# Two attention layers and a sign layer on one core: row stores, first score operands, adjacency padding and five sums of products moved

## The chip, the cores and the metric

One core of a Trainium2 chip. The metric is the device time of one execution in microseconds. The engines are named as the profile names them: PE (TensorE's matmuls; PEld, its weight loads), DVE (VectorE), ACT (ScalarE), POOL (GpSimd), SP (SyncE, which here only issues DMA transfers; SPq is its queue).

## The reference

x is 3327 x 512, adj a 3327 x 3327 matrix of zeros and ones. Two attention layers with residual, a layer norm, then a layer of signs, another residual and another layer norm:

```
for l in range(2):                                   # h starts as x
    Wh, Ws = split(h @ W_stack[l])                   # 3327 x 512 each
    a = softmax(Wh @ Ws.T, axis=-1) * adj
    h = leaky_relu(a @ Wh + h, 0.01)
x = layernorm(x + h)
ba, bw = (x > 0), sign(weight)
out = layernorm(x + relu(adj @ (ba @ bw.T)))
```

## The kernel before

**Tiles.** The 3327 rows are 26 tiles of 128 (the last has 127 rows), 13 pairs of tiles (`q`, `g`) and 7 chunks of four tiles (`c`; the last chunk has two). Every large product is done in Strassen's way: seven half-size products instead of eight, from sums of blocks that DVE or POOL make (`left_sums`, `right_sums`: four operations each).

**Projection** (`project`, lines 285 to 488). Chunk by chunk, PE makes `wsT` and then `whT`, each a "weave" of two chains of seven products. `weave` (line 222) takes several lists and emits their entries in the order of (i + 0.5) / length, so that other work stands between the products. Into the weave of chunk c+1's `wsT` goes the list `rest` of chunk c: the sums of the scores' right operands (`queries`, stored by POOL as `gs_d`) and, for each tile, `turn_rows` (line 417): two DVE transpositions (line 422) into a buffer `wr`, of which there are three, and at once four stores of it on SP (line 427). Into the weave of `whT` goes `keys` (the scores' left operands, stored by POOL as `xs_d`) and, for the first six value pairs, `sum_values`: four DVE sums of rows that `begin_values` loaded back with three transfers on SP; two POOL stores keep the result in `ws_d`. Pairs 0 and 1 are loaded after chunk 1, 2 and 3 after chunk 2, 4 and 5 after chunk 3, and summed a chunk later. The first chunk of layer 0 is turned by PE (`transpose_first`); weights are put in place by ACT (`part_w`).

**Attention** (`attention`, lines 499 to 1081). The loop variable v counts the pairs (g, q) whose values are being multiplied; u = v + 30 counts half steps of the scores, which run 30 steps ahead. Before v = 0 PE does scores only: 14 products for each q of a chunk, from `gs` (seven blocks for a chunk, two buffers) and `xs` (for each q two tiles, `xs0` and `xs1`, two buffers each, loaded by `load_xs`, line 515). The first `gs` is loaded at u = -4 in one transfer of 1792 KB, each `xs` two half steps ahead. Then DVE subtracts the column maximum (`off`), ACT takes the exponential, DVE multiplies with the adjacency (`masked`), POOL makes four sums (lines 738 to 741, `as`), and PE multiplies with the values (line 765). `load_adj` (line 659) loads 256 x 256 blocks of adj into four buffers; where a block reaches past column 3326 (g = 12) or row 3326 (q = 12), POOL first sets the missing part to zero (lines 664 and 666), and the last tile's load comes in pieces of 128, 112 and 15 rows. A list `early` places other work at given v: the value pairs that projection did not do (the last seven, `begin_values` and `sum_values`, lines 913 and 917), and in layer 0 the next layer's weights and first four tiles of x, at the end (lines 968 to 976).

**The end of layer 1.** From v = 130 on, `load_products` (line 1085) loads the sign layer's operands `xw` and, at v = 158 to 168, calls `product_sums` (line 1109) for pairs 0 to 10: four DVE subtractions each, written over the values `wh[p]` that are no longer needed. PE does parts of the last product (`aggregate`) between the values. `finale` does the rest.

**What sets the order.** Both functions run under a manual schedule: within each, every engine runs its instructions in the order in which the program emits them. Only where projection and attention meet does the scheduler merge the two orders.

Of the kernel before, what the change touches and what calls it, by code (L numbers as in the profile page):

```python
# [30 lines left out]
def kernel(  # L31
# [199 lines left out]
    ch_lane, acc_lane = (ps_ch, "ch"), (ps_acc, "acc")  # L231
    w_rows, wb_of, wsum_of, spare_of, x_first, sums_first = ({} for _ in range(6))
    ROWS = 6

# [32 lines left out]
    def right_x(c, xT, t):  # L267
# [7 lines left out]
        )  # L275

    def load_values(l, q, b12):

        nc.sync.dma_start(out=wh[q][:, 0], in_=wh_d[l][2 * q][:, :HD])
        nc.sync.dma_start(  # L280
            out=wh[q][:, 1:3], in_=wh_d[l][2 * q + 1].rearrange("p (a n) -> p a n", a=2)
        )
        nc.sync.dma_start(out=b12, in_=wh_d[l][2 * q][:, HD:])

    def project(l, pre):
# [3 lines left out]

        def load_x(c, tiles=None):  # L290
            if c >= NC:
                return
            for t in tiles or tiles_of(c):
                some = src[t * P : t * P + rows(t), :]
                if c == 0:
                    xt = slot([P, D], F32, f"xr_{l}_{t}")
                    load_rows(nc.sync, xt, some, rows(t))
                else:
                    xt = slot([P, P // B, P], F32, f"xr_{l}_{t}")
                    if rows(t) < P:  # L300
                        nc.gpsimd.memset(xt[:, rows(t) // B :], 0.0)
                    load_laid(nc.sync, xt, some, rows(t))
                rows_of.setdefault(c, []).append(xt)

        def transpose_first(lane):

            pool, tag = lane
            xTs[0] = pre.tile([P, KD, CW], F32, tag="xT", bufs=2, name=f"xT_{l}_0")
            pts = [pool.tile([P, CW], F32, tag=tag, name=f"pxt_{l}_{k}") for k in range(KD)]
            xts = [t.rearrange("r (p k) -> r k p", k=KD) for t in rows_of[0]]  # L310

            for a in range(CT):
                for k in range(KD):
                    nc.tensor.transpose(pts[k][:, ts(a, P)], xts[a][:, k], ident)
            for k in range(KD):
                copy_out(k, xTs[0][:, k], pts[k])

        def transpose_x(c, a):
# [20 lines left out]
        if l == 0:  # L339
            load_x(0, (0, 1))  # L340
            load_w(l, 1, (0, 1))
            load_x(0, (2, 3))
            load_w(l, 1, (2, 3))
            load_w(l, 0)
            spare_of[l] = ops.tile([P, 14, HW], F32, tag="gs", name=f"spare_{l}")
            wsum_of[l] = ops.tile([P, 4, 2, HD], F32, tag="gs", name=f"wbsum_{l}")
            wb_of[l] = m[:, 0:2], m[:, 2:4]
        else:
            xTs[0] = x_first[l]
            of_x[0] = sums_first[l]  # L350
# [66 lines left out]
        def turn_rows(t, lo, hi):  # L417
# [3 lines left out]
            for side, half in enumerate((lo, hi)):  # L421
# [3 lines left out]
                )  # L425
            for a in range(P // B):
                nc.sync.dma_start(
                    out=wh_d[l][t][:, ts(a, P)].rearrange("(r v) f -> v r f", v=B),
                    in_=wr[ts(a, B)],
                )  # L430

# [13 lines left out]

        rows34 = {}
        weights = [lambda k=k: part_w(l, 0, k, wa[:, k]) for k in range(KD)] + left_w(of_a)
        if l == 0:
            transpose_first(acc_lane)
            for k in range(KD):  # L450
                part_w(l, 1, k, m[:, k])
            t, b = sums_x(0), left_w(of_b)
            for do in t[:2] + b[:2]:
                do()
            weights = [b[2], t[2], b[3], t[3]] + weights
        else:
            weights += [
                lambda e=e: nc.scalar.copy(m[:, 2 * e : 2 * e + 2], wb_of[l][e]) for e in range(2)
            ]
        rest = []  # L460
        for c in range(NC):
# [12 lines left out]
            later = []  # L474
            old = [q for q in (2 * c - 4, 2 * c - 3) if 0 <= q < ROWS]
            turns += [lambda q=q: sum_values(q) for q in old]
            chains, made = products(c, "whT", of_a)
            weave(*chains, rest, turns)
            rest = queries(c, made)
            for a, e in enumerate(made):  # L480
                rest += [
                    lambda t=t, e=e: turn_rows(t, *e) for t in half_tiles(c * CT // 2 + a)
                ]
            for q in (2 * c - 2, 2 * c - 1):
                if 0 <= q < ROWS:
                    begin_values(q)
        for do in rest:
            do()

# [9 lines left out]
    def attention(l, att):  # L499
# [4 lines left out]
        ahead = [(c, q, s) for c in range(NC) for q in range(NQ) for s in range(2)]  # L504
        sc, top, total, off, adj, acc, gs, xs, ch = ({} for _ in range(9))
        asum, ws, out_, early = {}, {}, {}, {}
        WS = 3

        def load_gs(c, i, n=1):
            if i == 0:  # L510
                gs[c] = ops.tile([P, 7, 2, HW], F32, tag="gs", bufs=2, name=f"gs_{l}_{c}")
            if i <= (T3 if len(halves_of(c)) == 2 else B21):
                nc.sync.dma_start(out=gs[c][:, i : i + n], in_=gs_d[l][c][:, i : i + n])

        def load_xs(c, q):
            if len(halves_of(c)) == 2:
                groups = (S1, 4), (A22, 3)
            else:
                groups = (A11, 4),
            for i, (a, n) in enumerate(groups):  # L520
                t = ops.tile([P, 4 - i, 2, P], F32, tag=f"xs{i}", name=f"xs{i}_{l}_{c}_{q}")
                nc.sync.dma_start(out=t[:, :n], in_=xs_d[l][q][:, a : a + n])
                for e in range(n):
                    xs[c, q, a + e] = t[:, e]

        def product(c, q, bank, a, b, start):
# [3 lines left out]
            for k in range(2):  # L530
                nc.tensor.matmul(  # L531
                    ch[bank], xs[c, q, a][:, k], gs[c][:, b, k],
                    start=(start and k == 0), stop=(k == 1), skip_group_check=True,
# [87 lines left out]
        def column_max(g):  # L621
# [27 lines left out]
            def back():  # L649
# [4 lines left out]
                    whole.unsqueeze(2).to_broadcast([P, w, B]),  # L654
                )

            return [(-0.04, fold), (0.2, turn), (0.5, across), (0.7, back)]

        def load_adj(g, q):
            i0, n = half_cols(g)  # L660
            at = att.tile([P, 2, HW], F32, tag="adj", bufs=4, name=f"adj_{l}_{g}_{q}")
            adj[g, q] = at
            if n < HW:
                nc.gpsimd.memset(at[:, :, n:], 0.0)
            if rows(2 * q + 1) < P:
                nc.gpsimd.memset(at[:, 1], 0.0)
            if rows(2 * q + 1) == P:
                nc.sync.dma_start(
                    out=at[:, :, :n],
                    in_=adjT[2 * q * P : (2 * q + 2) * P, i0 : i0 + n].rearrange(  # L670
                        "(a p) i -> p a i", p=P
                    ),
                )
                return
            for a in range(2):
                j = 2 * q + a
                load_rows(
                    nc.sync, at[:, a, :n],
                    adjT[j * P : j * P + rows(j), i0 : i0 + n], rows(j),
                )  # L680

# [242 lines left out]

        for n, q in enumerate(range(ROWS, NQ)):
            at = 1 - LOOK + 4 * n
            assert at + 2 < 1 - WS
# [15 lines left out]
        else:  # L943
# [26 lines left out]

            place(end + 3, 0.9, lambda: load_w(l + 1, 1))
            place(end + 4, 0.2, begin_w)
# [7 lines left out]
            for i in range(4):  # L980
                place(end + 10 + i, 0.65, lambda: parts.pop(0)())
            place(n - 10, 0.95, lambda: load_w(l + 1, 0))
            for a in range(CT):
                place(n - 9 + a, 0.9, lambda a=a: load_first(a))
                place(n - 5 + a // 2, 0.45, lambda a=a: turn_x(x_first[l + 1], a, laid.pop(0)))
# [18 lines left out]
        for v in range(-LOOK - 4, len(steps)):  # L1004
# [6 lines left out]
            if v + 4 in blocks and (v + 4 < 0 or blocks[v + 4] != steps[v + 4]):  # L1011
                load_adj(*blocks[v + 4])
            if 0 <= u + 2 < len(ahead):
                c, q, h = ahead[u + 2]
                if h == 0:
                    load_xs(c, q)
            if u == -4:
                load_gs(0, 0, 7)

# [31 lines left out]
            if last:  # L1051
                load_products(v)
        if not last:
# [23 lines left out]
    JL = 2  # L1077
    NS = -(-NQ // JL)
    EARLY = NQ - 2
    XH = NT // 2  # L1080
# [3 lines left out]

    def load_products(v):

# [15 lines left out]
        p = v - NQ * (NQ - 1) - 2  # L1102
        if 0 <= p < EARLY:
            product_sums(p)
        n = v - NQ * NQ + 3 * NS
        if 0 <= n < 3 * NS:
            load_aggregate(*divmod(n, NS))

    def product_sums(p):
        x1, x2 = xw[2 * p], xw[2 * p + 1]  # L1110
        xt[p] = wh[p].bitcast(F16).rearrange("p a n -> p (a n)")[:, : 4 * HD].rearrange(
            "p (i n) -> p i n", i=4
        )
        for do in right_sums(
            x1[:, :HD], x1[:, HD:], x2[:, :HD], x2[:, HD:], *(xt[p][:, i] for i in range(4))
        ):
# [9 lines left out]
    def aggregate(g, b, p, i):  # L1126
# [9 lines left out]
        else:  # L1136
            of = (t[:, 1], t[:, 2], t[:, 0], x2[:, HD:], t[:, 3])[i - 2]

# [234 lines left out]
```

## Time and profile before

| | us |
|---|---|
| median of 3 runs | 2627.83 (2625.72 to 2629.0) |
| the profiled execution's own time | 2627.48 |
| its span in the trace | 2625.7 |
| PE, PEld busy | 2554.6, 2227.5 |
| DVE, POOL, ACT busy | 2141.6, 1095.4, 802.9 |
| projection of layer 0, up to its last product | 0 to 187 |
| attention of layer 0 | 187 to 1240 |
| projection of layer 1 | 1227 to 1411 |
| attention of layer 1 | 1411 to 2487 |
| rest of the sign layer, up to PE's last matmul | 2487 to 2605.1 |

The page gives busy time per engine; since PE is busy most of the span, the views to read are those that tell when it is not: who waited for whom, and the instructions in order of time around each pause, where the number in brackets is the idle time before an instruction and what ended it. A mean granted clock below 1 in a stretch says that PE ran more slowly there. DMA transfers are issued by SP and POOL in the order of their queues; the trace gives each one's issue and its landing.

### The profile page before, as it was taken

The numbers are of one execution on the slowest core, as the hardware profiler recorded it, in microseconds if no ns is written. First come the engines' busy times: TensorE is split into PE (matmuls) and PEld (weight loads), VectorE is DVE, ScalarE is ACT, GpSimd is POOL, SyncE is SP. The second block draws the span as 40 slices with busy tenths as digits, with TensorE's granted clock in tenths as the row PEclk, the third lists the DMA queues.
The fourth block names the chain that finished last, engine by engine and source line by source line (L and its number), as shares of the span: only waits on it lengthen the run. The fifth ranks groups of instructions, "written<-read, shape, count | busy, mean of one in ns | idle before, by whom it ended". The sixth has DMA issues, their size and how long they took to land. (4 is left out here: it accounts for less than half of the span.)

```text
span 2625.7 us, 40583 instructions
## 1 busy us (share of the span) xinstructions
PE 2554.6 (97%) x12456; PEld 2227.5 (85%) x12456; DVE 2141.6 (82%) x4528; ACT 802.9 (31%) x1986; POOL 1095.4 (42%) x2030
## 2 busy tenths in 40 slices
PE   8979999999999999999998999999999999999998
PEld 7868788888888888887887888888888888888787
DVE  6866888889898888759884888988889888877977
ACT  3323333323333323223322333333323333222143
POOL 3441343444444444557452144444444444455611
PEclk9999999999999999999998999999999999999999
DMA  6888776777777777668788977777787777778775
GB/s 202 302 267 297 267 259 233 249 249 251 249 244 255 242 240 239 233 226 270 227 298 272 345 235 261 236 269 248 247 273 244 265 250 243 247 265 272 260 258 185
DMA packets 366348, 667.77 MB, mean 254 GB/s; under 512 B 52761, under 2 KB 222579, under 8 KB 365868
## 3 DMA queue, kind: packets, MB, share of 16 engines
q1 hardware_dynamic: 329596, 556.00, 65.0%
q0 software_dynamic: 36528, 109.10, 11.0%
q8 instruction: 102, 1.67, 0.3%
q14 instruction: 122, 1.00, 0.1%
HBM read 541.75 MB, written 123.19 MB: 253 GB/s over the span
## 5 line engine op out<-in xcount | busy, mean ns | idle before, releaser
L531 PE MATMUL pZ<-gs,xs 128*128 128x256 f32 x2496 | 640.9, 381 | 30.2 <-DVE whT L190 14.1
L531 PEld LDWEIGHTS pZ<-gs,xs 128*128 128x128 f32 x2496 | 474.7, 191 | 99.4 <-DVE whT L190 14.5
L738 POOL TENSOR_TENSOR as<-s 128x128 f32<-128x128 f32 x338 | 163.3, 483 | 823.5 <-DVE s L700 646.0
L765 PE MATMUL acc<-ws,s 128*128 128x256 f32 x1352 | 402.1, 379 | 0.0
L765 PE MATMUL acc<-wh,s 128*128 128x256 f32 x1352 | 355.9, 379 | 0.9 <-DVE s L700 0.8
L765 PE MATMUL acc<-ws,as 128*128 128x256 f32 x1352 | 348.1, 380 | 8.3 <-POOL as L740 5.6
L531 PE MATMUL pY<-gs,xs 128*128 128x256 f32 x1248 | 320.4, 379 | 0.0
L690 ACT ACTIVATE s<-s 128x512 f32<-128x512 f32 x338 | 213.4, 631 | 283.4 <-DVE s L684 282.2
L765 PEld LDWEIGHTS acc<-ws,as 128*128 128x128 f32 x1352 | 255.9, 190 | 47.2 <-POOL as L740 9.4
L765 PEld LDWEIGHTS acc<-wh,s 128*128 128x128 f32 x1352 | 256.5, 190 | 37.1 <-DVE s L700 2.4
L765 PEld LDWEIGHTS acc<-ws,s 128*128 128x128 f32 x1352 | 256.0, 190 | 34.5
L601 DVE TENSOR_TENSOR top<-top,s 128x512 f32<-128x512 f32 x286 | 199.7, 711 | 82.6 <-ACT s L588 54.3
L531 PEld LDWEIGHTS pY<-gs,xs 128*128 128x128 f32 x1248 | 236.9, 190 | 32.6 <-ACT p L548 0.3
L684 DVE TENSOR_TENSOR s<-s,off 128x512 f32<-128x512 f32 x338 | 248.9, 736 | 0.6
L700 DVE TENSOR_TENSOR s<-s,adj 128x512 f32<-128x512 f32 x338 | 238.3, 705 | 10.2 <-POOL as L740 1.5
L695 DVE TENSOR_TENSOR total<-total,s 128x512 f32<-128x512 f32 x312 | 230.8, 740 | 0.0
L548 ACT COPY u<-pZ 128x256 f32<-128x256 f32 x312 | 115.9, 371 | 358.5 <-PE pZ L531 357.9
L740 POOL TENSOR_TENSOR as<-s 128x128 f32<-128x128 f32 x338 | 201.8, 597 | 26.5
L765 PE MATMUL acc<-wh,as 128*128 128x256 f32 x676 | 201.2, 379 | 0.0
L739 POOL TENSOR_TENSOR s<-s 128x128 f32<-128x128 f32 x338 | 188.6, 558 | 26.5
L741 POOL TENSOR_TENSOR as<-s,as 128x128 f32<-128x128 f32 x338 | 180.2, 533 | 26.5
L573 DVE TENSOR_TENSOR s<-p,u 128x256 f32<-128x256 f32 x156 | 66.4, 426 | 131.0 <-ACT u L548 130.4
(224 smaller groups left out, 3858.8 us busy)
## 6 DMA issues: line engine op xcount, KB each, us to landing
ws<-ws_d SPq DMA_DIRECT2D x338, 512.0 KB, 3.7
xs<-xs_d SPq DMA_DIRECT2D x182, 512.0 KB, 6.0
adj<-in_adjT_dram SPq DMA_DIRECT2D x315, 256.0 KB, 4.3
xs<-xs_d SPq DMA_DIRECT2D x156, 384.0 KB, 6.5
gs<-gs_d SPq DMA_DIRECT2D x74, 256.0 KB, 5.4
adj_d<-ab POOLq DMA_DIRECT2D x169, 112.0 KB, 4.1
ahl<-adj_d SPq DMA_DIRECT2D x78, 224.0 KB, 4.6
xs_d<-s POOLq DMA_DIRECT2D x52, 256.0 KB, 3.6
```

Source lines behind the costliest of these rows:

```text
L531: nc.tensor.matmul(ch[bank], xs[c, q, a][:, k], gs[c][:, b, k], start=(start and k == 0), stop=(k == 1), skip_group_check=True,)
L548: nc.scalar.copy(ch[name], ch[bank])
L601: nc.vector.tensor_tensor(top[i], top[i], t, ALU.max)
L684: nc.vector.tensor_tensor(s, s, off[g].to_broadcast([P, 2, HW]), ALU.subtract)
L690: nc.scalar.activation(sc[g, q], sc[g, q], AF.Exp)
L695: nc.vector.tensor_tensor(total[g], total[g], sc[g, q], ALU.add)
L700: nc.vector.tensor_tensor(s, s, adj[g, q], ALU.mult)
L738: nc.gpsimd.tensor_tensor(s3, a11, a21, ALU.subtract)
L739: nc.gpsimd.tensor_tensor(a21, a21, a22, ALU.add)
L740: nc.gpsimd.tensor_tensor(s2, a21, a11, ALU.subtract)
L741: nc.gpsimd.tensor_tensor(s4, a12, s2, ALU.subtract)
L765: nc.tensor.matmul(acc[g][i // 2][:, i % 2], a[i], b[i], start=(q == 0 and i % 2 == 0), stop=(q == NQ - 1), skip_group_check=True,)
```

## The change

- **Row stores.** `turn_rows` only puts its store on a list; a new entry `store_rows` after it in `rest` issues it, on SP as before. `rest` has 10 entries instead of 6. After the last chunk the stores go to POOL's queue.
- **Value pairs.** Projection does five pairs instead of six: pair c-1 is loaded after chunk c and pair c-2 summed in chunk c. Attention does the other eight, 3 or 4 steps apart instead of 4.
- **First operands of the scores.** `gs` of the first chunk, in seven transfers, and `xs` of q = 0 and 1 are loaded in projection, after chunk 5 of 0 to 6, and no longer in attention. They are emitted before the list with chunk 5's row stores.
- **Adjacency.** No memsets. A block that reaches past the last column is loaded in full width from the flat matrix, so that its last column holds the start of the next row; `off` of that column gets 1e30 by a DVE memset, and since `off` is subtracted the exponential there is zero. The last pair's second tile comes in 112, 14 and 1 rows and a row that fills the padding, and one element more where g = 12: five or six transfers instead of three.
- **Sums of products.** Pairs 0 to 4 are done at v = 143, 145, ... 151 in other buffers; pairs 5 to 10 stay at v = 163 to 168.
- **Start.** Layer 0 loads the four x tiles and then the weights, instead of two and two in turn; `part_w` of a weight follows the copy of the same index.
- **Layer 0's end.** The next layer's weights are loaded one tile per step (from v = 155 and v = 160) instead of four at once at 155 and 159; its four x tiles at v = 155, 157, 159 and 161 instead of 160 to 163.

```diff
-    ROWS = 6
+    ROWS = NC - 2
...
             for k in range(KD):
                 copy_out(k, xTs[0][:, k], pts[k])
+                part_w(l, 1, k, m[:, k])
...
-            load_x(0, (0, 1))
-            load_w(l, 1, (0, 1))
-            load_x(0, (2, 3))
-            load_w(l, 1, (2, 3))
+            load_x(0)
+            load_w(l, 1)
...
-            for a in range(P // B):
-                nc.sync.dma_start(
-                    out=wh_d[l][t][:, ts(a, P)].rearrange("(r v) f -> v r f", v=B),
-                    in_=wr[ts(a, B)],
-                )
+            def store(eng):
+                for a in range(P // B):
+                    eng.dma_start(
+                        out=wh_d[l][t][:, ts(a, P)].rearrange("(r v) f -> v r f", v=B),
+                        in_=wr[ts(a, B)],
+                    )
+            turned.append(store)
+
+        def store_rows(eng=nc.sync):
+            while turned:
+                turned.pop(0)(eng)
...
-            old = [q for q in (2 * c - 4, 2 * c - 3) if 0 <= q < ROWS]
-            turns += [lambda q=q: sum_values(q) for q in old]
+            if 0 <= c - 2 < ROWS:
+                turns.append(lambda: sum_values(c - 2))
...
-                rest += [
-                    lambda t=t, e=e: turn_rows(t, *e) for t in half_tiles(c * CT // 2 + a)
-                ]
-            for q in (2 * c - 2, 2 * c - 1):
-                if 0 <= q < ROWS:
-                    begin_values(q)
+                for t in half_tiles(c * CT // 2 + a):
+                    rest += [lambda t=t, e=e: turn_rows(t, *e), store_rows]
+            if 0 <= c - 1 < ROWS:
+                begin_values(c - 1)
+            if c == NC - 2:
+                gs_of[l] = ops.tile([P, 7, 2, HW], F32, tag="gs", name=f"gs_{l}_0")
+                for i in (B11, B21, T1, T2, B22, T3, T4):
+                    nc.sync.dma_start(out=gs_of[l][:, i], in_=gs_d[l][0][:, i])
+                for q in range(2):
+                    load_xs(l, 0, q)
         for do in rest:
-            do()
+            do() if do is not store_rows else do(nc.gpsimd)
...
+                if half_cols(g)[1] < HW:
+                    nc.vector.memset(off[g][:, 0, half_cols(g)[1] :], -FAR)
...
-            if n < HW:
-                nc.gpsimd.memset(at[:, :, n:], 0.0)
-            if rows(2 * q + 1) < P:
-                nc.gpsimd.memset(at[:, 1], 0.0)
...
+            nc.sync.dma_start(out=at[:, 0], in_=some(j1, P))
+            cut = r - r % 16
+            nc.sync.dma_start(out=at[:cut, 1], in_=some(j2, cut))
+            nc.sync.dma_start(out=at[cut : r - 1, 1], in_=some(j2 + cut, r - 1 - cut))
+            nc.sync.dma_start(out=at[r - 1 : r, 1, :n], in_=some(j2 + r - 1, 1, n))
+            if n < HW:
+                nc.sync.dma_start(out=at[r - 1 : r, 1, n:], in_=some(j2 + r - 2, 1)[:, n:])
+            nc.sync.dma_start(out=at[r:, 1], in_=some(j2, P - r))
...
-            at = 1 - LOOK + 4 * n
+            at = 1 - LOOK + 7 * n // 2
...
-            place(end + 3, 0.9, lambda: load_w(l + 1, 1))
+            for k in range(KD):
+                place(end + 3 + k, 0.9, lambda k=k: load_w(l + 1, 1, [k]))
+                place(end + 8 + k, 0.9, lambda k=k: load_w(l + 1, 0, [k]))
...
-            place(n - 10, 0.95, lambda: load_w(l + 1, 0))
             for a in range(CT):
-                place(n - 9 + a, 0.9, lambda a=a: load_first(a))
+                place(n - 14 + 2 * a, 0.9, lambda a=a: load_first(a))
...
-            if 0 <= u + 2 < len(ahead):
+            if 4 <= u + 2 < len(ahead):
                 c, q, h = ahead[u + 2]
                 if h == 0:
-                    load_xs(c, q)
-            if u == -4:
-                load_gs(0, 0, 7)
+                    load_xs(l, c, q)
...
-        if 0 <= p < EARLY:
+        if SOON <= p < EARLY:
             product_sums(p)
+        p, odd = divmod(v - first[0] - XH, 2)
+        if 0 <= p < SOON and not odd:
+            product_sums(p, att)
...
+        if p < SOON:
+            tags = (("xs1",), ("xs1",), ("top1",), ("p1", "u2"), ("p5", "u3"))[p]
...
+                t = pool.tile([P, n, HD], F16, tag=tag, bufs=2 if tag == "xs1" else 1,
+                              name=f"xsum_{p}_{tag}")
```

Here SOON = 5, NC = 7, NQ = XH = 13, `first[0]` = 130, and `some` takes rows of the flat adjacency in full width.

## The prediction

> **What bounds the kernel now.** I read the page's busy times first.
>
> ```profile
> PE 2554.6 (97%) x12456; PEld 2227.5 (85%) x12456; DVE 2141.6 (82%) x4528; ACT 802.9 (31%) x1986; POOL 1095.4 (42%) x2030
> ```
>
> TensorE is idle for 2625.7 - 2554.6 = 71.1 us. The chain of waits shows its last matmul ending at 2605.1, so 20.6 us of that is a tail that no edit touches. The other 50 us, and time at a lower clock, are all that this change can win: it removes no matmul. Next, who PE waited for (total, times, longest):
>
> ```profile
> PE pZ L531 <- DVE whT L190: 14.1, 2, 7.3
> PE pZ L531 <- DMA xs<-xs_d: 13.1, 6, 5.7
> PE pX_wsT L370 <- DVE whT L190: 5.7, 4, 2.6
> PE pxt L314 <- DMA xr<-in_x_dram: 5.7, 2, 3.8
> PE acc L765 <- POOL as L740: 5.6, 7, 1.2
> ```
>
> The first two rows are four pauses, at the two passages from projection to attention: 7.29 us before 182.15 and 5.74 before 198.52 in layer 0, 6.79 before 1404.89 and 4.45 before 1421.22 in layer 1. The timelines of VectorE and of SyncE's queue say why (start, duration):
>
> ```profile
> 180.89 1.08 DVE L422 STREAM_TRANSPOSE wr<-whT 128x256 f32<-128x256 f32 x2 [8.87 <-DMA wh_d<-wr]
> ```
>
> ```profile
> 161.61 0.34 SPq L513 DMA_DIRECT2D gs<-gs_d  x1
> 162.00 1.71 SPq L522 DMA_DIRECT2D xs<-xs_d  x2
> ...
> 169.47 23.80 SPq L427 DMA_DIRECT2D wh_d<-wr  x24
> 193.32 0.93 SPq L522 DMA_DIRECT2D xs<-xs_d  x2
> ```
>
> Chunk 5's row stores are queued behind the first `gs` (1792 KB) and `xs` (896 KB). A store lands in a median 2.1 us, here in up to 10.2. The fourth turned tile needs a `wr` buffer, of which there are three, and VectorE stands 8.87 us; behind it stands the addition that PE waits for. Then SP must issue eight more stores, chunk 6's, before q=1's `xs` at 193.32: the second pause. The pauses also cost clock (columns: stretch, length, five engines' busy time, granted clock, DMA share, GB/s):
>
> ```profile
> 165.00:181.00 16.00, 9.86 (x89) 9.66 (x87) 6.57 (x17) 4.63 (x17) 5.51 (x10) 0.93 0.99 376
> 179.00:186.00 7.00, 3.85 (x18) 3.68 (x19) 3.03 (x10) 0.53 (x2) 1.96 (x3) 0.53 0.74 229
> 196.00:203.00 7.00, 4.48 (x11) 3.66 (x12) 0.42 (x1) 0.37 (x1) 0.00 (x0) 0.52 0.80 299
> 1400.00:1411.00 11.00, 6.11 (x27) 5.93 (x27) 4.43 (x13) 0.80 (x3) 5.18 (x10) 0.53 0.86 289
> ```
>
> At about half clock, half of PE's busy time is lost: 1.8, 2.1 and 3.0 us, and 1.7 after 1421. With the pauses, passage 0 costs 7.3 + 1.8 + 5.7 + 2.1 = 16.9 us, passage 1 6.8 + 3.0 + 4.5 + 1.7 = 16.0.
>
> **The change, part by part** (gain positive).
>
> *Passages.* Seven `gs` loads and two q's `xs` (2 x 896 KB) now stand on SP at the end of chunk 5, still ahead of its stores; ahead of them come the three loads of value pair 4 (512 KB). q=1's `xs` no longer waits for chunk 6's stores, so the second pause goes: 5.7 + 2.1, and 4.5 + 1.7. What is late next are chunk 5's stores. Pair 4's loads can use 161 to 165, where only 242 GB/s moved; the added 917,000 bytes of `xs` cannot, since DMA is 0.99 busy after that. At all 376 GB/s they take 2.4 us, at half of it, beside POOL's writes, 4.9; I take 3, nearer the first, because POOL's writes are finite and only trade places. VectorE's wait, and PE's, grow by that; half a microsecond more of slow clock in passage 0. Gain 7.8 - 3.5 = 4.3 and 6.2 - 3 = 3.2. Bounds: -2 each (delay 8) to 16.9 and 16.0 (all cured).
>
> *Stores a turn later.* Nothing else in the woven lists issues on SP, so SP's order of stores stays: 0. The woven list grows from 6 to 10 entries, so the first transposition moves from 0.42 to 0.25 of a 12 us weave and the fourth from 0.92 to 0.85, 2.0 and 0.8 us earlier; bounds +-0.8, as VectorE's other additions slide against them. Chunk 6's eight stores move to POOL: 8 x 0.54 = 4.3 us there, covered, since POOL has nothing from 190 to 208.9; uncovered they would delay one `ws_d` store that is read tens of us later.
>
> [...] POOL's own writes issued at 169 to 177 do share the 0.99. [...]
>
> *Value pairs.* Projection loads one pair per chunk for five chunks instead of two for three. In chunks 2 to 4 VectorE does 4 x 0.42 = 1.7 us less and SP three loads less ahead of the stores for which VectorE waited 4.96 us at 103 and 5.21 at 131. PE's pauses there are 0.9 + 0.5 + 2.6, plus 1.7 of clock (141 to 145 has 0.57), 5.7 in all; layer 1 has 0.3 + 0.5 + 1.9 + 0.5 = 3.2. Chunks 5 and 6 get 1.7 us more. I take about half: 3.0 and 1.5 (0 to all). The pair moved into attention costs 1.7 us of VectorE, which is busy 13.3 of 18 us there: hidden. Its 1 MB of DMA meets 0.95 to 1.00 of DMA at 222 to 258: at 359 GB/s 2.9 us of transfers, with `xs` landing 4 to 7 us after its issue and a turn of products lasting 6 us. I take -0.5 per layer (0 to -2.9).
>
> [...]
>
> *Start.* Four x tiles, then weights. PE stood 3.8 us and again 1.9 for x tiles 2 and 3, which come two transfers sooner; `part_w` then starts before the second copy, and ScalarE's copies (0.55 and 1.1 us) decide. 11.42 becomes about 9, but the second product still needs all four weights: 1.8 (0.5 to 2.5).
>
> *Memsets.* 69 POOL instructions go: 39 x 0.10 + 30 x 0.33 = 14 us on an engine with room. What counts is who waits for them.
>
> ```profile
> 255.83 5.00 SPq L117 DMA_DIRECT2D adj<-in_adjT_dram  x2
> ```
>
> ```profile
> 259.08 0.54 POOL L923 DMA_DIRECT2D ws_d<-wn  x1 [8.03 <-DVE wn L209]
> 259.61 0.54 POOL L723 DMA_DIRECT2D adj_d<-ab  x1
> 260.14 0.33 POOL L666 MEMSET adj<- 128x256 f32 x1
> ```
>
> SP's second load waits for the memset, the memset for a POOL store, that for VectorE; `xs` is then late and PE stands 1.3 us at 268.77: gained (0 to 1.3). The 30 last-pair loads get two or three transfers more, 0.43 us of SP each, under 30 us in 2625 with SP waiting between; a memset of one column of `off` per layer is about 0.1 on VectorE. Both 0 (to -1).
>
> *Layer 0's end.* Of PE's pauses at 1180 to 1230, 1.8 us are `ws` landing late behind the bunched loads of weights and x, now one per step or every second step, and 0.8 a POOL memset: 2.6 (0 to 3.6). The 2.5 us before `pz` is POOL's own sum, which stays.
>
> *Five sums of products.*
>
> ```profile
> 2370.00:2415.00 45.00, 45.00 (x211) 38.87 (x210) 32.63 (x52) 10.26 (x21) 23.59 (x40) 1.00 0.77 261
> ...
> 2445.00:2485.00 40.00, 34.34 (x164) 25.77 (x163) 37.17 (x76) 6.80 (x12) 25.79 (x48) 1.00 0.76 264
> ```
>
> At 2445 to 2485 VectorE (third number) is the limit and PE stands 5.7 us. One pair's four subtractions take 1.3 to 2.1 us; five pairs are 8 us. They go to steps 143 to 151, about 2370 to 2415, where VectorE has 12 us free in gaps of 3.8 and PE none. Their tiles are free by then (chunk 6 uses no `xs1`, `p1`, `p5`, `u2`, `u3`). Six pairs stay, and `ws` loads at 346 to 379 GB/s may become the limit: 4.5 (2 to 5.8).
>
> **Sum:** 1.8 + 3.0 + 4.3 + 1.3 - 1.0 + 2.6 + 1.5 + 3.2 + 4.5 = 21.2 us. The profiled execution took 2627.48 (span 2625.7), 0.35 below the median 2627.83. 2627.5 - 21.2 = **2606**. Its own range, with partly offsetting misses of +-10: 2596 to 2618.
>
> **Rivals.**
> 1. *The passages are cured.* If chunk 5's stores land before the fourth transposition wants a buffer, 16.9 + 16.0 replace 4.3 + 3.2: 2581. For it: the transpositions come earlier. Against: the stores have more bytes ahead of them, not fewer. 0.15.
> 2. *The wait moves and is paid again.* The `xs` delay is 8 us per passage (-2 each), projection's pauses return in chunks 5 and 6 (0 and 0), the start brings 0.5, and the rest stays: 0.5 - 4 + 1.3 - 1.0 + 2.6 + 4.5 = 3.9, so 2624. 0.13.
> 3. *Slower.* One mechanism: the stores behind 4.2 MB. Without store delay the sum is 21.2 + 6.5 = 27.7; it is used up when the stores land 13.9 us later per passage. For the added 917,000 bytes that means 66 GB/s, a third of the 188 that gave 4.9 us above. If pair 4's loads delay the stores in full too, 1.44 MB at 80 GB/s come to 18 us per passage: 27.7 - 36 = -8, so 2635. 0.10.
> 4. *The main case*, 0.62.
>
> Changes of 0.2% (5.3 us) are about what a measurement tells from none. Faster: 0.62 + 0.15 = 0.77; same 0.13; slower 0.10. The range 2580 to 2627 leaves out rival 3 and the lower half of rival 1; the sums of all bounds, 2572 and 2637, lie outside it, because the bounds are not all met at once.
>
> **What would show it.** Right: no PE pause for `xs` at about 198 and 1421; one PE pause per passage, of 9 to 11 us, ended by VectorE's `whT` addition, with VectorE waiting for a `wr` store; no L664 or L666, and SP not held at the last pair's `adj`; under 2 us of PE pauses in the last twelve steps; the first ws product near 9. Wrong: passage pauses under 3 us (rival 1) or over 15 (rival 3), PE waiting for `xs` between 220 and 260, or pauses over 3 us still in the last steps.

## The result and the profile after

The changed kernel takes 2606.98 us (median of 4 runs, 2602.07 to 2611.5) against 2628.22 for the kernel before: ratio 0.992, 95% interval 0.9901 to 0.994. The forecast was 2606. The profiled execution took 2611.5 us (span 2609.7), 4.5 above the median; that of before took 2627.48.

The page's busy line, then the longest waits of PE (total, times, longest):

```profile
PE 2546.4 (98%) x12431; PEld 2228.1 (85%) x12456; DVE 2142.5 (82%) x4530; ACT 804.2 (31%) x1986; POOL 1090.3 (42%) x1975
```

```profile
PE pZ L545 <- DVE whT L190: 28.7, 2, 14.7
PE pxt L328 <- DMA xr<-in_x_dram: 5.2, 2, 3.9
PE pX L545 <- DVE s L593: 3.2, 2, 1.6
PE acc L791 <- POOL as L766: 2.8, 4, 0.9
PE pz L842 <- POOL total L833: 2.4, 1, 2.4
```

The `pX_wsT` row of before (projection, 5.7 us) is gone, and so are the pauses for `xs` at the passages. The two rows that named the adjacency's memsets are gone too, but the longer of them, 2.5 us ahead of `pz`, stands on as a wait of 2.4 us for GpSimd's own sum. And the first row has doubled, from 14.1 to 28.7. The timelines of PE, of VectorE and of SP's queue around the first passage:

```profile
183.23 1.22 PE L545 MATMUL pZ<-gs,xs 128*128 128x256 f32 x2 [14.08 <-DVE whT L190]
```

```profile
181.97 1.08 DVE L435 STREAM_TRANSPOSE wr<-whT 128x256 f32<-128x256 f32 x2 [14.19 <-DMA wh_d<-wr]
```

```profile
157.77 6.39 SPq L508 DMA_DIRECT2D gs<-gs_d  x7
164.21 4.09 SPq L287 DMA_DIRECT2D xs<-xs_d  x4
169.18 16.15 SPq L441 DMA_DIRECT2D wh_d<-wr  x16
189.02 0.34 SPq L297 DMA_DIRECT2D wn<-wh_d  x1
192.04 8.95 SPq L287 DMA_DIRECT2D xs<-xs_d  x4
```

Read the two ends of the pause. PE restarts at 183.23, against 182.15 before: one microsecond later. It stopped at 169.15 instead of 174.86, nearly six sooner, since the projection runs without pauses now. The pause ends when a store has landed and so frees a buffer, and that store did not come sooner with PE. The clock follows (stretch, length, five engines' busy time, granted clock, DMA share, GB/s):

```profile
171.00:188.00 17.00, 4.77 (x20) 4.59 (x21) 5.12 (x16) 0.53 (x2) 3.68 (x7) 0.50 0.86 304
1389.00:1407.00 18.00, 6.25 (x27) 6.07 (x28) 5.86 (x17) 0.80 (x3) 5.32 (x9) 0.53 0.86 304
...
2430.00:2470.00 40.00, 38.19 (x192) 31.21 (x195) 37.49 (x64) 7.55 (x13) 29.95 (x44) 1.00 0.85 288
```

The last line answers to 2445:2485 before: PE has 38.2 of 40 us there instead of 34.3.

**Where the gain lies.** PE does the same 12456 weight loads in every kernel here, in nearly one order. The start of the n-th one in the trace of before, less that in another kernel's trace, is how far this kernel is ahead at that point; the growth from one point to the next is its gain in that segment. The segments end at 31.2 (start), 170.0 (projection 0), 230.6 (passage 0), 1169.8 (attention 0), 1223.9 (layer end 0), 1391.8 (projection 1), 1456.0 (passage 1), 2400.4 (attention 1), 2489.2 (the last steps) and 2616.1 us of before. One profiled execution each, us, positive is faster. Segments with the same instructions as before show up to 2 us either way (projection 0 in sums_only and no_memsets_only: 2.0 and 1.7). Among the kernels with the changed start, the start goes from -0.8 to 2.7 and attention 1 from -3.8 to 2.2; the -4.3 in late_and_gpsimd's rest has no explanation here.

| kernel | start | proj 0 | pass 0 | attn 0 | end 0 | proj 1 | pass 1 | attn 1 | last steps | rest |
|---|---|---|---|---|---|---|---|---|---|---|
| forecast | 1.8 | 3.0 | 4.3 | 0.8 | 2.6 | 1.5 | 3.2 | -0.5 | 4.5 | 0 |
| the changed kernel | -0.8 | 6.5 | 0.5 | 1.7 | -0.4 | 4.7 | -1.7 | 1.6 | 5.3 | -0.4 |
| pairs_only | 0.4 | 6.5 | 0.5 | 1.6 | -0.1 | 4.3 | -2.4 | -0.1 | 0.0 | -0.9 |
| stores_only | 0.3 | 0.3 | 9.0 | 0.6 | -1.7 | -0.2 | 3.9 | -1.0 | 0.3 | 0.1 |
| sums_only | 0.2 | 2.0 | 1.4 | -0.4 | 1.2 | -1.1 | 0.2 | -1.4 | 3.4 | 0.1 |
| no_memsets_only | -0.2 | 1.7 | 0.8 | 1.5 | -1.4 | -0.9 | -0.6 | -0.7 | 0.0 | 0.1 |
| own_buffer | 1.1 | 6.5 | 4.5 | 1.7 | 0.1 | 4.7 | 1.2 | 0.5 | 5.3 | 0.1 |
| operands_late | 2.7 | 6.5 | 2.6 | 1.7 | 0.3 | 4.9 | 2.8 | 0.5 | 5.3 | 0.1 |
| buffer_and_late | 1.0 | 6.5 | 3.1 | 1.7 | 0.7 | 4.7 | 3.4 | 0.2 | 5.3 | 0.1 |
| no_own_buffers | 2.0 | 6.5 | 1.6 | 1.7 | 0.6 | 4.5 | 0.2 | 2.2 | 5.3 | -0.1 |
| late_and_gpsimd | 1.6 | 6.5 | 11.5 | 1.5 | -0.3 | 4.0 | 11.0 | 1.6 | 5.2 | -4.3 |
| early_own_gpsimd | 1.0 | 6.5 | 12.1 | 1.2 | 0.1 | 4.7 | 11.3 | -3.8 | 5.3 | -0.9 |
| start_undone | -1.2 | 6.5 | 13.8 | 0.1 | 0.0 | 4.9 | 12.5 | -3.0 | 5.3 | -0.2 |
| layer_end_undone | 1.9 | 6.5 | 12.4 | 1.3 | -1.0 | 4.4 | 11.8 | -0.8 | 5.3 | 0.1 |

### The profile page after: what moved, and what is told of

Same layout as the page of the kernel before. It is cut to its first block, busy times and chain, and to the rows that moved or that the text cites. A ratio compares the mean times of both kernels' runs of the same rounds, so it can differ in the third digit from the quotient of the medians.

```text
span 2609.7 us, 40621 instructions
## 1 busy us (share of the span) xinstructions
PE 2546.4 (98%) x12431; PEld 2228.1 (85%) x12456; DVE 2142.5 (82%) x4530; ACT 804.2 (31%) x1986; POOL 1090.3 (42%) x1975
## 4 chain that ended last, share of the span: by engine, by line
PE 89%; DMA 4%; DVE 3%; SPq 1%; issue 1%; POOL 1%; ACT 0%; DVEq 0%; POOLq 0%; ACTq 0%
PE acc L791 36%; PE pZ L545 20%; PE pY L545 10%; PE pX L545 5%; PE agg L1179 4%; PE pD L545 3%; PE pZ_wsT L383 3%; PE pZ_whT L383 3%; PE pY_whT L383 1%; PE pY_wsT L383 1%; DMA wh_d<-wr 1%; PE pX_wsT L383 1%; DMA gs<-gs_d 1%; PE pxw L910 1%; PE pX_whT L383 1%
## 5 line engine op out<-in xcount | busy, mean ns | idle before, releaser
L545 PE MATMUL pZ<-gs,xs 128*128 128x256 f32 x2496 | 638.5, 380 | 30.8 <-DVE whT L190 28.7
```

The lines of the kernel that those rows point to most:

```text
L545: nc.tensor.matmul(ch[bank], xs[l, c, q, a][:, k], gs[c][:, b, k], start=(start and k == 0), stop=(k == 1), skip_group_check=True,)
```

## The experiments

The first four ask which part of the change gives what, and what holds the passage. Times are medians; ratios are to the kernel before in the same comparison, with their 95% intervals.

**own_buffer.** The changed kernel with the turned rows of the last two chunks in buffers of their own.

```diff
-            wr = pre.tile([P, P // B, P], F32, tag="wr", bufs=3, name=f"wr_{l}_{t}")
+            if t < (NC - 2) * CT:
+                wr = pre.tile([P, P // B, P], F32, tag="wr", bufs=3, name=f"wr_{l}_{t}")
+            else:
+                wr = slot([P, P // B, P], F32, f"wr_{l}_{t}")
```

> The changed kernel, with chunk 5's and 6's turned rows in six further buffers, so that no transposition waits for a store. Queue theory (the pause of 14 us per passage is VectorE waiting for a buffer whose store lies behind the operands in SP's queue): no VectorE wait for wr near 182, PE pauses under 3 us per passage, about 2575 us. Bandwidth theory (the passage has more bytes than about 400 GB/s move between 158 and 180, and the operands themselves are not there before about 176): the pause becomes 5 to 8 us and is ended by the landing of gs or xs, about 2588 us.

2602.93 us, 0.9895 (0.9879 to 0.9912): slower than either theory said (2575 and 2588). In the changed kernel's trace the DMA engines moved 386 GB/s from 158 to 180, at a share of 1.03, and 417 from 170 to 179. VectorE no longer stands for a buffer at the passage, but the pause comes back later, for the `xs` of q = 2:

```profile
193.04 2.05 PE L548 MATMUL pZ<-gs,xs 128*128 128x256 f32 x4 [8.91 <-DMA xs<-xs_d]
```

In SP's queue those loads stand behind chunk 5's sixteen stores, which keep SP from 165.79 to 188.14. A second hold stood behind the first.

**operands_late.** The changed kernel with the first `gs` and `xs` loaded in attention again; chunk 6's stores stay on GpSimd.

```diff
-            if c == NC - 2:
-                gs_of[l] = ops.tile([P, 7, 2, HW], F32, tag="gs", name=f"gs_{l}_0")
-                for i in (B11, B21, T1, T2, B22, T3, T4):
-                    nc.sync.dma_start(out=gs_of[l][:, i], in_=gs_d[l][0][:, i])
-                for q in range(2):
-                    load_xs(l, 0, q)
...
-            if 4 <= u + 2 < len(ahead):
+            if 0 <= u + 2 < len(ahead):
...
+            if u == -4:
+                load_gs(0, 0, 7)
```

> The changed kernel with the first gs and xs loaded in attention again, as before the change; chunk 6's rows still go to POOL. If the early xs of q=1 and the split gs are what lengthened the first pause (from 7 to 14 us), it comes back to 7 to 10 us, the second pause is at most 3 us because chunk 6's stores are off SP's queue, and the time is 2598 to 2606 us. If loading early is what removed the second pause, that pause is back with 4 to 6 us and the time is 2608 to 2614 us.

2602.49 us, 0.9897 (0.9881 to 0.9914). One pause per passage, 12.09 and 11.94 us, more than the 7 to 10 expected, and none for `xs`:

```profile
177.75 1.22 PE L538 MATMUL pZ<-gs,xs 128*128 128x256 f32 x2 [12.09 <-DMA wh_d<-wr]
```

So the early loads weren't needed to remove the second pause; without them it stays away, and the passages are 2.1 and 4.5 us shorter (2.6 and 2.8 in the table against 0.5 and -1.7). The early loads lengthen the first pause by 2.0 and 2.7 us (14.08 and 14.65 with them). Two things that can keep the second pause away remain in this kernel: chunk 6's stores are not in SP's queue, and a long first pause covers the loads. The next two runs have one of them each.

**pairs_only.** The kernel before, with only the value pairs moved.

```diff
-    ROWS = 6
+    ROWS = NC - 2
...
-            old = [q for q in (2 * c - 4, 2 * c - 3) if 0 <= q < ROWS]
-            turns += [lambda q=q: sum_values(q) for q in old]
+            if 0 <= c - 2 < ROWS:
+                turns.append(lambda: sum_values(c - 2))
...
-            at = 1 - LOOK + 4 * n
+            at = 1 - LOOK + 7 * n // 2
```

> The kernel before with the value pairs alone moved: one pair per chunk, five in projection, eight in attention. If these pairs are what kept projection waiting, PE's pauses before 145 fall from 4 us to under 1.5 us with no slow clock there, layer 1 likewise, and the passages give part of it back: 2619 to 2625 us. If the spacing of the transpositions is, the pauses stay and the time is 2626 to 2630 us.

2617.75 us, 0.9957 (0.994 to 0.9974). The projections gain 6.5 and 4.3 us, nearly all of what the changed kernel gains there (6.5 and 4.7). PE's timeline shows what the first passage does with it:

```profile
180.43 1.22 PE L530 MATMUL pZ<-gs,xs 128*128 128x256 f32 x2 [12.54 <-DMA wh_d<-wr]
196.51 1.10 PE L530 MATMUL pZ<-gs,xs 128*128 128x256 f32 x4 [1.51 <-DMA xs<-xs_d]
```

The restart moved from 182.15 to 180.43, though PE came 7.0 us sooner, and the pause grew from 7.29 to 12.54 (in layer 1 from 6.79 to 14.11). The second pause shrank from 5.74 to 1.51, as SP's stores could go on meanwhile. For the passage the trade is about even in layer 0 (0.5) and costs 2.4 us in layer 1.

Why did the end of the pause not come sooner with PE? It does so elsewhere: sums_only, below, has the passage of before and reached it 2.3 us earlier in its execution, and its pause ended 3.6 us earlier (178.60), after 6.00 us. From one and the same weight load of PE to the end of the pause, first in sums_only, then in pairs_only:

```profile
139.26:178.60 39.34, 32.81 (x193) 29.58 (x193) 28.32 (x69) 10.97 (x34) 20.92 (x35) 0.96 0.93 318
135.25:180.43 45.18, 32.65 (x194) 29.74 (x192) 27.25 (x66) 11.33 (x35) 20.17 (x34) 0.90 0.92 315
```

PE's busy time (32.8 and 32.7 us) and the rate of the DMA engines (318 and 315 GB/s) are about the same; the bytes, rate times length, are 12.5 and 14.2 MB. Pair 4's loads, pair 3's stores by GpSimd and one `xs` now fall into this stretch, 512 KB each. At this rate they take 5 us by estimate, near what the pause grew by. That they are the cause fits in size; no run moves these transfers alone.

**stores_only.** The kernel before, with only the stores issued a turn later and chunk 6's by GpSimd.

```diff
-                nc.sync.dma_start(
-                    out=wh_d[l][t][:, ts(a, P)].rearrange("(r v) f -> v r f", v=B),
-                    in_=wr[ts(a, B)],
-                )
+            turned.append(store)
...
-                rest += [
-                    lambda t=t, e=e: turn_rows(t, *e) for t in half_tiles(c * CT // 2 + a)
-                ]
+                for t in half_tiles(c * CT // 2 + a):
+                    rest += [lambda t=t, e=e: turn_rows(t, *e), store_rows]
         for do in rest:
-            do()
+            do() if do is not store_rows else do(nc.gpsimd)
```

> The kernel before with the row stores alone put a turn later (ten entries in the woven list, chunk 6's stores on POOL). If order on SP's queue decides the second pause, it falls from 5.7 and 4.5 us to under 2 us, the first pause stays within 1 us of 7, and the time is 2616 to 2622 us. If the spacing also frees projection, its pauses fall too and the time is 2610 to 2616 us. If neither, 2626 to 2630 us.

2613.65 us, 0.9934 (0.9917 to 0.995). The first pause is 4.50 us (4.19 in layer 1), not within 1 us of 7 as expected; the second is down to 0.25 in layer 0, but still 3.65 in layer 1:

```profile
178.77 1.22 PE L537 MATMUL pZ<-gs,xs 128*128 128x256 f32 x2 [4.50 <-DVE whT L190]
```

The passages gain 9.0 and 3.9 us, the largest single gain of the change. It does not add to that of the pairs: 11.9 us (2629.67 - 2617.75) and 16.0 (2629.67 - 2613.65) alone, while the changed kernel, with the other parts too, is 21.2 below before.

**sums_only.** The kernel before, with only five pairs' sums of products moved.

```diff
-        if 0 <= p < EARLY:
+        if SOON <= p < EARLY:
             product_sums(p)
+        p, odd = divmod(v - first[0] - XH, 2)
+        if 0 <= p < SOON and not odd:
+            product_sums(p, att)
```

> The kernel before, with only the sums of products of five pairs moved into the last stretch of layer 1's attention. If the PE pauses at the end of layer 1 are VectorE work in the wrong place, as the prediction has it and the trace of the changed kernel bears out (5.0 us), this alone gains 4 to 6 us: 2623 to 2626. If the pauses were only pushed from one place to another and the gain of the changed kernel there came from its earlier arrival, it gains less than 2 us: 2628 to 2630. Every passage and every projection should stand as before.

2625.57 us, 0.9991 (0.9977 to 1.0006): the whole kernel's time does not decide it. The segment does: 3.4 us in the last steps here, 5.2 to 5.3 in every kernel that has this part with the others.

**no_memsets_only.** The kernel before, with only the adjacency's memsets gone and the wider loads in their place.

```diff
-            if n < HW:
-                nc.gpsimd.memset(at[:, :, n:], 0.0)
-            if rows(2 * q + 1) < P:
-                nc.gpsimd.memset(at[:, 1], 0.0)
```

> The kernel before, with only the memsets of the adjacency gone (GpSimd's, with the wider adjacency loads and VectorE's memset of the offsets in their place). The pause for xs at 268 and those at 1745, 1907 and 2069 should go (1.9 and 2.6 us in the changed kernel's trace against that of before): 2624 to 2627. Rival: the wider loads delay other operands by as much, and the time stays within 2 us of before: 2627 to 2631. If GpSimd's load were what holds the end of layer 0 back, the ws pauses near 1205 would go too and 2 us more would be gained; the changed kernel speaks against it.

2626.75 us, 0.9989 (0.9979 to 1.0): within what can be told from no change. Attention 0 gains 1.5 us, and the pause at 268 is gone; of the pauses for `xs` in layer 1 that were expected to go, the one at 1745 is longer than before (1.38 against 0.78). pairs_only and stores_only have no pause at 268 either, with the memsets in place (1.6 and 0.6 in attention 0), and start_undone, without memsets, gains 0.1 there. So what the memsets alone are worth isn't shown.

**buffer_and_late.** own_buffer and operands_late together.

> The changed kernel with both edits tried before together: the turned rows of the last two chunks in buffers of their own, and the scores' first operands loaded where they were before. Theory of bytes: with the DMA engines full from 158 to 180, what matters is how many bytes stand ahead of the scores' operands. The rows' buffers no longer hold VectorE, so the first products start at about 171, but the operands of the second pair now stand behind chunk 5's stores and land near 187: a pause of 3 to 6 us per passage instead of 12, 2594 to 2599. Theory of the buffer alone: no pause over 3 us is left at either passage and no half clock there, 2580 to 2588. If the two edits do not add up, because each already takes away the same wait: 2600 to 2604.

2602.91 us, 0.9899 (0.9877 to 0.9922): no better than either. The timelines of SP and of PE:

```profile
162.38 23.21 SPq L444 DMA_DIRECT2D wh_d<-wr  x16
185.69 0.39 SPq L287 DMA_DIRECT2D xs<-xs_d  x1
```

```profile
191.04 2.04 PE L541 MATMUL pZ<-gs,xs 128*128 128x256 f32 x4 [9.68 <-DMA xs<-xs_d]
```

q = 1's second `xs` tile is issued at 185.69, after sixteen stores that took SP 23.21 us (1.45 us each; the median of SP's 2022 issues in before is 0.42); PE waits until 191.04. The theory of bytes expected 3 to 6 us of pause, that of the buffer none: both fell. What fits is a queue: the loads wait to be issued. In these 23 us SP itself waited for earlier transfers to land, 10.4 us in the two longest rows of its waits:

```profile
SPq L444 <- DMA xs<-xs_d: 6.6, 3, 3.2
...
SPq L444 <- DMA wh_d<-wr: 3.8, 4, 1.1
```

In the trace of before SP issues a transfer only after the one eight places ahead of it has landed, without exception among the 2014 that have one. For instance, the stores issued at 175.20 and 177.22 follow the landings, at 175.18 and 177.21, of the `xs` loads eight places ahead. A late store thus holds up SP's whole queue.

**late_and_gpsimd.** buffer_and_late, with chunk 5's stores issued by GpSimd too.

```diff
-                    rest += [lambda t=t, e=e: turn_rows(t, *e), store_rows]
+                    put = (lambda: store_rows(nc.gpsimd)) if c == NC - 2 else store_rows
+                    rest += [lambda t=t, e=e: turn_rows(t, *e), put]
```

> The kernel of buffer_and_late, with chunk 5's stores issued by GpSimd as well, so that SP's queue is free for the second pair's operands. If only the bytes count, the stores take the same room on the DMA engines and the time is within 3 us of buffer_and_late. If it is SP's queue (the operands wait to be issued behind sixteen stores), the pause for xs goes: 4 to 8 us below buffer_and_late. Against it: GpSimd has its own stores of xs and gs to issue there and would hold these back, a loss of 2 to 5 us.

2590.18 us, 0.9847 (0.9825 to 0.987), 12.7 us below buffer_and_late and the step that cures the passages: 11.5 and 11.0 in the table. All four `xs` tiles of the first two pairs leave before 158:

```profile
154.38 3.54 SPq L287 DMA_DIRECT2D xs<-xs_d  x4
```

Stretch 160 to 230, first of the changed kernel, then of this one:

```profile
160.00:230.00 70.00, 55.92 (x299) 50.58 (x299) 37.03 (x94) 19.20 (x60) 20.55 (x36) 0.88 0.92 317
```

```profile
160.00:230.00 70.00, 65.61 (x340) 57.29 (x339) 44.02 (x118) 23.25 (x71) 28.05 (x50) 1.00 1.01 368
```

PE is busy 65.6 us instead of 55.9, at full clock (1.00), with the DMA engines busier (1.01 against 0.92). So full DMA engines alone do not stop PE here; it stops when a transfer that it needs next is late (9.68 us for `xs` in buffer_and_late).

**no_own_buffers.** late_and_gpsimd with the three shared buffers back (the edit of own_buffer undone).

> late_and_gpsimd with the turned rows of chunks 5 and 6 back in the three shared buffers: late loads and GpSimd's stores alone. Theory of two holds in a row (VectorE held by the rows' buffers first, the second pair's operands held in SP's queue second): the first hold comes back, VectorE waits for a store that GpSimd has issued no sooner than SP did, PE pauses 8 to 14 us per passage, and the time is 2600 to 2608. Theory of SP's queue alone: the buffers free as soon as the stores flow, the pause stays under 3 us, and the time is 2588 to 2594.

2606.96 us, 0.9921 (0.9904 to 0.9937). The first hold is back, though GpSimd issues the stores. VectorE's timeline:

```profile
178.30 1.08 DVE L435 STREAM_TRANSPOSE wr<-whT 128x256 f32<-128x256 f32 x2 [14.34 <-DMA wh_d<-wr]
```

PE pauses 13.18 and 13.73 us. Two holds in a row is what these runs show. With late operands and neither cure the time is 2602.49 (operands_late), with own buffers alone 2602.91 (buffer_and_late: the second hold), with GpSimd's stores alone 2606.96 (the first), and with both 2590.18.

**early_own_gpsimd.** late_and_gpsimd with the first operands loaded a chunk sooner, as in the change (the edit of operands_late undone).

> late_and_gpsimd with the scores' first operands loaded a chunk sooner again, as the changed kernel does. Theory of two holds: nothing is left that these loads could free, and they only stand ahead of each other; the time is within 3 us of late_and_gpsimd, 2588 to 2594. Theory that the early loads themselves cost DMA time ahead of chunk 5's last work (2.4 to 3 us per passage was the difference of operands_late against the changed kernel): 2594 to 2598.

2589.7 us, 0.985 (0.9833 to 0.9866), equal to late_and_gpsimd; passages 12.1 and 11.3. Once nothing holds the queue, it makes no difference when these loads are issued.

**start_undone.** late_and_gpsimd with the start of before.

```diff
-            load_x(0)
-            load_w(l, 1)
+            load_x(0, (0, 1))
+            load_w(l, 1, (0, 1))
+            load_x(0, (2, 3))
+            load_w(l, 1, (2, 3))
...
                 copy_out(k, xTs[0][:, k], pts[k])
-                part_w(l, 1, k, m[:, k])
```

> late_and_gpsimd with the start as before: x and the weights loaded in turns of two tiles, the weights' parts after all four copies. By the prediction the changed start is worth 1.8 us (0.5 to 2.5): 2591 to 2593 here. The changed kernel's profiled execution showed 0.8 us lost instead, with a half clock to 17.5 us against 14.9; the three runs with the same start since then show 1.2 to 3.1 gained. If the start decides nothing: within 1 us of late_and_gpsimd.

2590.98 us, 0.9861 (0.9844 to 0.9877): the same. The start itself loses 2.8 us against late_and_gpsimd (-1.2 and 1.6), and passage 0 gains 2.3 more (13.8 against 11.5; the other two kernels of this kind have 12.1 and 12.4). Whether the passage gives back what the start brings can't be told from one execution each.

**layer_end_undone.** late_and_gpsimd with the loads at the end of layer 0 as before.

```diff
-            for k in range(KD):
-                place(end + 3 + k, 0.9, lambda k=k: load_w(l + 1, 1, [k]))
-                place(end + 8 + k, 0.9, lambda k=k: load_w(l + 1, 0, [k]))
+            place(end + 3, 0.9, lambda: load_w(l + 1, 1))
...
-                place(n - 14 + 2 * a, 0.9, lambda a=a: load_first(a))
+            place(n - 10, 0.95, lambda: load_w(l + 1, 0))
+            for a in range(CT):
+                place(n - 9 + a, 0.9, lambda a=a: load_first(a))
```

> late_and_gpsimd with the loads at the end of layer 0 as before: the weights in one load each, and the next layer's first rows one step apart instead of two. The prediction gave this part 2.6 us, by way of the pauses for ws near 1205: 2592 to 2594 here. The changed kernel's trace still has these pauses (1.05 and 1.21 us), so that I now expect under 1 us of difference: 2589 to 2591, with the pauses for ws about as long as in late_and_gpsimd (1.1 us). If the spread loads are what keeps other loads in time, pauses of 2 us or more for ws or the first rows come up between 1180 and 1225.

2587.71 us, 0.9844 (0.9831 to 0.9858): not slower, the lowest median of all. The spread loads bring nothing that can be seen; PE's pauses for `ws` between 1180 and 1225 are 1.7 us in all here, 1.1 in late_and_gpsimd, and 2.3 in the changed kernel against 1.8 before.

## Why the prediction was right, and where it wasn't

The total came out: 21.2 us forecast, 21.2 in the medians. It came out by misses that offset each other, though: 7.5 us too little for the two projections and the sums of products together, 8.7 too much for the two passages. That is luck, not accuracy. The profiled execution alone gained 16.0 by its times (2627.48 - 2611.5).

- **Projection: right in kind, forecast at half the size.** Taken at half, 3.0 and 1.5, as the pauses were expected to come back in chunks 5 and 6; measured 6.5 and 4.7. pairs_only has 6.5 and 4.3, so the value pairs alone give nearly all of it. The pauses do not return in the projection. The 1.7 us of slow clock counted after the 2.6 us pause that ends at 140.63 is not in every execution (last section), so part of the 6.5 depends on the one execution of before.
- **Passages: the step that failed.** "I take 3, nearer the first [...] VectorE's wait, and PE's, grow by that": PE's pause grew by 6.8 us (7.29 to 14.08) and 7.9 (6.79 to 14.65). That is outside the 9 to 11 us given as the sign of being right and just short of the 15 of the slower rival; the gain was 0.5 and -1.7 instead of 4.3 and 3.2. The term that was priced, the early `xs`, was about right: operands_late puts the early loads at 2.0 and 2.7. What was put at nothing is the moved pairs' traffic ("Pair 4's loads can use 161 to 165"; GpSimd's stores of pair 3 are not in the sum): with the pairs alone moved the pause grows by 5.3 and 7.3 (pairs_only). Rival 3 had the pair's loads as a delay. Projection and passage together were forecast at 7.3 and 4.7 and came to 7.0 and 3.0: the pairs' gain in the projection was for a good part paid again at the passage.
- **Stores a turn later: a term that wasn't zero.** stores_only, which has this and chunk 6's stores on GpSimd, shortens the first pause by 2.8 and 2.6 us; chunk 6's stores come after that pause. Bounds of 0.8 either way were given. Two kernels with the stores of before have 6.00 and 6.54 in layer 0 (sums_only, no_memsets_only), so about 1 us of it may be chance.
- **The second pause: right effect, cause right in part.** It went as said, and order on SP was given as the cause. But the early loads of `xs`, which were to change that order, weren't needed (operands_late), and chunk 6's stores on GpSimd alone leave 3.65 us of it in layer 1 (stores_only).
- **Rival 1, "the passages are cured", 2581,** was too large for what the cure brings here: late_and_gpsimd gains 11.5 and 11.0 in the passages, about two thirds of the 32.9 us, and reaches 2590. The change itself reaches neither condition: three shared buffers still hold VectorE, and behind them sixteen stores still hold SP's queue.
- **Start: open in size.** 1.8 forecast, -0.8 in the changed kernel's profiled execution, 1.0 to 2.7 in the seven others with this start. In that one PE did 18 matmuls in 7.20 us from 10 to 18 (clock 0.57), in own_buffer, with the same start, 25 in 7.97. The changed kernel's first `ws` product comes at 9.95 (9 was the sign given). By start_undone the total hardly depends on the start.
- **Memsets: open.** 1.3 forecast; attention 0 gains 1.7, but the pause that was to go is absent from kernels with the memsets too (no_memsets_only, above). The eighth value pair in attention cost nothing that the table shows (-0.5 per layer forecast); no pause for `xs` came up between 220 and 260.
- **Layer 0's end:** 2.6 forecast, -0.4 measured. The memset's pause of 0.8 us is gone, but those for GpSimd's sums are 1.3 us instead of 0.6. The `ws` pauses are 2.3 us instead of 1.8; layer_end_undone shows no sign that they came from the bunched loads.
- **Sums of products:** 4.5 forecast, 5.3 measured. The two stretches chosen, early with VectorE free and late with VectorE the limit, were read rightly: sums_only gains 3.4 there with this edit alone.
- **Slips in the working:** the row of 13.1 us for `xs` is six waits, of which the two at the passages make 10.2. A delay of 8 us leaves -0.7 and -1.8 in the two passages, not -2 each, so rival 2 comes to 2622 by its own terms. And 2606 with 10 us either way is 2596 to 2616, not 2618.

## What to carry to other kernels

Before adding gains, mark the points whose time is set by a transfer and not by the busiest engine. Work that moves takes its transfers with it: here the moved value pairs freed the projection and lengthened the pause behind it, and a sum that prices only the first is too high. Where a wait goes, look through the same queue for the next instruction that waits behind the same stores. Here two holds stood in a row: in the kernel with late operands each cure alone gave nothing or cost 4.5 us, both together gave 12.3 (2602.49 to 2590.18). Compare the same instruction's start in both traces, segment by segment: a total that agrees can hide terms that don't.

## What the runs showed of the hardware

Moving the stores between queues changes more than the order. The DMA queues from 170 to 185 (packets, MB, share), first of buffer_and_late, then of late_and_gpsimd:

```profile
q0 software_dynamic: 1326, 4.15, 74.4%
q1 hardware_dynamic: 2064, 1.31, 28.8%
```

```profile
q1 hardware_dynamic: 1091, 2.63, 51.8%
q0 software_dynamic: 980, 2.67, 45.8%
```

With stores on both, GpSimd's queue (q0) moved 4.15 MB in 1326 packets and SP's (q1) 1.31 in 2064. The stores' packets differ: in the trace of the changed kernel, which has both kinds, a 64 KB store of SP's goes in packets of 512 bytes (1708 of q1's 2557 packets from 170 to 185) and the same store of GpSimd's in packets of 4096 (q0 has 407 of these and 224 of 4 bytes from 189 to 200, and none of 512). In the second kernel SP's queue holds only loads there, 2.63 MB in 1091 packets, and the two queues move about the same (2.63 and 2.67 MB). No run here separates the packets from the order of issue; late_and_gpsimd changes both, and how much of its 12.7 us is due to each stays open. In buffer_and_late the sixteen stores of the first passage kept SP's queue for 23.21 us; with those of both passages on GpSimd the kernel is 12.7 us faster.

The clock at the start is not set by the program alone. From 10 to 18 us PE did 18 matmuls in 7.20 us of busy time in the changed kernel (granted clock 0.57), 25 in 7.97 in own_buffer and 33 in 7.49 in operands_late, all with the same start: 0.40, 0.32 and 0.23 us each. The view gives a clock of 1.00 for the last two, but also for before, where the eight products from 11.42 took 3.78 us and the eight from 15.03 only 1.89, so that figure can't be read alone at the start. Nor is the clock the same after similar pauses in the projection: 2.61 us in before and 2.63 in stores_only were followed by a granted clock of 0.79 from 139 to 147, those of 2.31 in no_memsets_only and 2.02 in sums_only by 1.00 (139 to 147 and 138 to 146). Whether the length of the pause decides can't be told from four executions.
